# State-space mixer of a perceiver: rows of B, C and x projected one per pair of states and copied a pair later, and the second repeat of x moved forward

## The chip, the cores and the metric

The kernel runs on one core of one Trainium2 chip. A core has TensorE (PE; its weight loads are shown apart as PEld), VectorE (DVE), ScalarE (ACT), GpSimd (POOL) and SyncE (SP), each with a queue of its own that it works off in order. The metric is the device time of one execution in microseconds (us), the median over several runs.

## The reference

The reference is a perceiver of four blocks: cross-attention over a context, self-attention and feed-forward layers of different kinds in turn, on an input of 2 x 256 tokens of width 256. The change lies in one of these layers, a mixer of the Mamba-2 kind:

```python
z, x, Bm, Cm, dtr = jnp.split(hidden_states @ W_in, ..., axis=-1)   # 512, 128, 128, 512, 64
x = silu(causal_conv4(x) + conv_b)
x  = repeat(x as 8 groups of 16, 4)        # 32 groups of 16 channels
Bg = repeat(Bm as 8 groups of 16, 4)       # 16 state columns for each group
Cg = Cm as 32 groups of 16
delta = softplus(dtr @ W_dt + 2.0 * dt_bias)
a  = exp(delta[..., None] * A)             # A = -exp(A_log)
bb = (delta * x)[..., None] * Bg[:, :, :, None, :]
h_t = a_t * h_(t-1) + bb_t                 # for each of 512 channels x 16 states
y  = einsum('blgpn,blgn->blgp', h, Cg)
y  = (y + D * x) * silu(z)
return y @ W_out
```

## The kernel before

The mixer is the function `l1_attn`. Tokens lie along the free axis (512: two batches of 256), channels along the 128 partitions, so the 512 channels make four *quarters* j = 0 to 3. All tiles are f32, and a matmul over 128 x 512 shows as two MATMUL records in the trace.

`project` (L1499) multiplies 128 columns of the input weights with the normed input (two matmuls, four records) into one PSUM bank of the tag "mm"; the tag has three banks, "tr" two, "dec" two and "acc" one. A tile of a tag takes one of the tag's banks, and the first matmul into it waits until the last reader of the bank's former tile is done.

Ahead of the loop stand, in source order: the low-rank steps of quarters 0 and 1 (`steps_of`, bank "dec"), an exponential over both, the Silu of x, the gate z of quarter 0, `repeat_x(0)` (x of quarter 0 spread over its 128 channels by a matmul with a 0/1 matrix, then copied by ScalarE to `xr`), `rows_of_columns(0)` (the rows of B and of C of quarter 0, two projections, each copied by ScalarE, to `bT` and `cT`), the other gates, the softplus polynomial of quarter 0 on VectorE (`deltas(0, True)`), the steps of quarters 2 and 3, their exponential (L1558), `repeat_x(1)` and the polynomial of quarter 1. In this part instructions need not run in source order: each engine's queue is put together by the framework.

Then comes the loop over 32 *pairs* of state columns, eight pairs a quarter. It runs from k = -2 to 32 as a pipeline, and here each engine's order is the one written down (`in_order` over PE, DVE, ACT and POOL). In one turn:

- `states(k)`: PE spreads two columns of C over the partitions into two "mm" banks (L1577, 32-row matmuls that run side by side); VectorE does two scans (L1609) and then multiplies each by its C column (L1611), which frees the bank.
- `b_columns(k + 2)`: PE spreads two columns of B into the two "tr" banks (L1577); ScalarE copies them to `spread` (L1585).
- `drives(k + 1)`: ScalarE makes two decays (L1594) into the two "dec" banks, which the scans of pair k read before; POOL multiplies `spread` by delta times x (L1596). One step of the softplus polynomial of quarters 2 and 3 follows (an addition on ScalarE, L1462, and a multiplication on POOL, L1463).
- one step of `made`, if there is one left: from k = -2 on, in turn rows of B and C of quarter 1, x of quarter 2, rows of quarter 2, x of quarter 3, rows of quarter 3. Each is projected by PE and copied by ScalarE in the same turn (L1533, L1536, L1537); five steps, so done at k = 2.
- `add_up(k - 1)`: PE adds the two weighed states of the pair before to the sum of the quarter (L1618, two full matmuls with the identity).

What needs what was made: B of quarter 1 is first spread at k = 6, C of quarter 1 at k = 8; x of quarter 2 is read by the last softplus step of that quarter at k = 10. Behind the loop the layer ends with a part of the next layer (`conv_hidden`) and the output projection.

Of the kernel before, what the change touches and what calls it, by code (L numbers as in the profile page):

```python
# [22 lines left out]
P = 128  # L23
# [246 lines left out]
class Perceiver:  # L270
# [1197 lines left out]
    def l1_attn(self, x):  # L1468
# [3 lines left out]
        nc = self.nc  # L1472
        T = NT * P
        with ExitStack() as s:
# [24 lines left out]
            def project(at, n):  # L1499
                ps = self.bank([n, T])  # L1500
                self.mm(ps, [(win[:, k, at : at + n], xnT[:, k, :]) for k in range(KC)])
                return ps
# [14 lines left out]
            def steps_of(j):  # L1517
                ps = self.bank([P, T], "dec")
                self.mm(ps, [(wdt[:, ts(j, P)], dtT)])
                nc.scalar.activation(low[:, j, :], ps, AF.Abs, bias=dt2[:, j : j + 1])  # L1520
                nc.scalar.activation(high[:, j, :], ps, AF.Relu, bias=dt2[:, j : j + 1])

            bT, cT = pool.tile([P, 4, T], F32, name="bT"), pool.tile([P, 4, T], F32, name="cT")
            xr = pool.tile([P, 4, T], F32, name="xr")
# [3 lines left out]
            dx, yz = high, low  # L1528

            def repeat_x(j):  # L1530
                ps = self.bank([P, T], "tr")
                self.mm(ps, [(mats["x"][:, ts(j, P)], xc.rearrange("p b l -> p (b l)"))])
                nc.scalar.copy(xr[:, j, :], ps)  # L1533

            def rows_of_columns(j):
                nc.scalar.copy(bT[:, j, :], project(640 + j * P, P))  # L1536
                nc.scalar.copy(cT[:, j, :], project(1152 + j * P, P))  # L1537

            def deltas(j, vector):
                yield from self.softplus(delta[:, j, :], low[:, j, :], high[:, j, :], vector)  # L1540
                engine = nc.vector if vector else nc.gpsimd
                yield lambda: engine.tensor_mul(dx[:, j, :], delta[:, j, :], xr[:, j, :])
# [4 lines left out]
            nc.scalar.activation(xc, xc, AF.Silu, bias=self.col("conv_b"))  # L1547
            steps = [*deltas(0, True)]
            nc.scalar.activation(zs[:, 0, :], project(0, P), AF.Silu)
            repeat_x(0)  # L1550
            rows_of_columns(0)
            for j in range(1, 4):
                nc.scalar.activation(zs[:, j, :], project(j * P, P), AF.Silu)
            for step in steps:
                step()
            steps_of(2)
            steps_of(3)
            nc.scalar.activation(low[:, 2:4, :], low[:, 2:4, :], AF.Exp, scale=-1.0)  # L1558
            repeat_x(1)
            for step in deltas(1, True):  # L1560
                step()
            later = iter([*deltas(2, False), *deltas(3, False)])
            made = iter([partial(f, j) for j in range(1, 4) for f in ([repeat_x] * (j > 1) + [rows_of_columns])])


            pairs = [(j, q, rs) for j in range(4) for q in range(4) for rs in ((0, 1), (2, 3))]
# [13 lines left out]
            def b_columns(k):  # L1580
                got = columns(mats["b"], bT, *pairs[k], "tr")
                spread[k] = []
                for ps in got:
                    spread[k].append(p4.tile([P, T], F32, name="spread", tag="spread"))
                    nc.scalar.copy(spread[k][-1], ps)  # L1585

            def drives(k):
                j, q, rs = pairs[k]
                decay[k], drive[k] = [], []
                for r, b in zip(rs, spread.pop(k)):  # L1590

                    a = fading[len(decay[k])]
                    n = 16 * j + 4 * r + q
                    nc.scalar.activation(behind_first(a), behind_first(delta[:, j, :]), AF.Exp, scale=neg_a[:, n : n + 1])  # L1594
                    decay[k].append(a)
                    nc.gpsimd.tensor_mul(b, dx[:, j, :], b)  # L1596
                    drive[k].append(b)
                step = next(later, None)
                if step is not None:
                    step()  # L1600

            def states(k):
                got = columns(mats["c"], cT, *pairs[k], "mm")
                weighed[k] = []

                for a, bb in zip(decay.pop(k), drive.pop(k)):
                    h = p4.tile([P, T], F32, name="state", tag="state")
                    weighed[k].append(h)
                    nc.vector.tensor_tensor_scan(h, a, bb, 0.0, ALU.mult, ALU.add)  # L1609
                for c, h in zip(got, weighed[k]):  # L1610
                    nc.vector.tensor_mul(h, c, h)  # L1611

            def add_up(k):
                j, q, rs = pairs[k]
                if k % 8 == 0:
                    sums[j] = self.acc([P, T])
                for i, h in enumerate(weighed.pop(k)):
                    nc.tensor.matmul(  # L1618
                        sums[j], self.ident, h, start=k % 8 == 0 and i == 0, stop=k % 8 == 7 and i == 1
                    )  # L1620
                if k % 8 == 7:
                    nc.vector.scalar_tensor_tensor(
                        yz[:, j, :], xr[:, j, :], self.col("ssm_d", j), sums[j], ALU.mult, ALU.add
                    )
                    nc.gpsimd.tensor_mul(yz[:, j, :], yz[:, j, :], zs[:, j, :])

            e = mybir.EngineType
            with self.in_order(e.PE, e.DVE, e.Activation, e.Pool):
                n = len(pairs)
                for a in fading:  # L1630
                    nc.vector.memset(by_batch(a)[:, :, 0:1], 0.0)
                for k in range(-2, n + 1):
                    if 0 <= k < n:
                        states(k)
                    if k + 2 < n:
                        b_columns(k + 2)
                    if 0 <= k + 1 < n:
                        drives(k + 1)
                    step = next(made, None)
                    if step is not None:  # L1640
                        step()
                    if k > 0:
                        add_up(k - 1)
                self.conv_hidden("tr", "tr", "dec")
                return self.linear(yz, wout, x)
# [1248 lines left out]
```

## Time and profile before

| what | value |
|---|---|
| median of 3 runs | 2466.13 us (2465.45 to 2467.29) |
| the profiled execution | 2463.28 us |
| its span (first to last instruction) | 2461.5 us |
| granted TensorE clock, mean over the span | 0.99 |
| the mixer in the span: normed input's first transposes to the last add-up | 1245.6 to 1412.1 us |
| first B columns of the pair loop | 1268.8 us |
| first C columns | 1281.2 us |
| first scan (VectorE) | 1281.3 us |

Busy times of some groups of the mixer:

| line, engine, what | count | busy us | mean ns |
|---|---|---|---|
| L1618 PE, add-up | 128 | 63.3 | 617 |
| L1577 PE, C columns | 128 | 36.6 | 640 |
| L1577 PE, B columns | 128 | 34.9 | 591 |
| L1609 DVE, scan | 64 | 76.3 | 1215 |
| L1611 DVE, multiply by C | 64 | 40.4 | 673 |
| L1585 ACT, copy of a B column | 64 | 34.5 | 589 |
| L1594 ACT, decay | 64 | 42.1 | 698 |
| L1596 POOL, drive | 64 | 80.1 | 1278 |

A group's mean is the duration of a single record. Records of one engine overlap by about a tenth of a microsecond, so the distance between the starts of two instructions, not the mean, says what one costs its engine. In the timeline a row gives start, length of the merged records, engine, line, operation, tiles and the number of records; in brackets the engine's idle time before it, and what ended it.

### The profile page before, as it was taken

The numbers are of one execution on the slowest core, as the hardware profiler recorded it, in microseconds if no ns is written. First come the engines' busy times: TensorE is split into PE (matmuls) and PEld (weight loads), VectorE is DVE, ScalarE is ACT, GpSimd is POOL, SyncE is SP. The second block draws the span as 40 slices with busy tenths as digits, with TensorE's granted clock in tenths as the row PEclk, the third lists the DMA queues.
The fourth block names the chain that finished last, engine by engine and source line by source line (L and its number), as shares of the span: only waits on it lengthen the run. The fifth ranks groups of instructions, "written<-read, shape, count | busy, mean of one in ns | idle before, by whom it ended". The sixth has DMA issues, their size and how long they took to land. (4 is left out here: it accounts for less than half of the span.)

```text
span 2461.5 us, 51429 instructions
## 1 busy us (share of the span) xinstructions
PE 2395.0 (97%) x20501; PEld 1612.3 (66%) x20501; DVE 1676.4 (68%) x3125; ACT 1363.8 (55%) x2588; POOL 916.4 (37%) x860
## 2 busy tenths in 40 slices
PE   8999999999999999999989999999999999999989
PEld 6865577777766666666733376555966666665678
DVE  5645578888877777777758864555258888855642
ACT  3434566666666666666656522433137777785612
POOL 0420066666666655555819722002021222210000
PEclk9999999999999999999999999999999999999989
DMA  8321433333342222222320011125850000004755
GB/s 306 108 88 69 144 91 99 96 99 96 98 131 78 66 67 69 70 70 70 109 106 1 1 77 57 69 82 208 313 184 2 2 2 2 2 2 143 243 221 219
DMA packets 92640, 243.61 MB, mean 99 GB/s; under 512 B 8072, under 2 KB 23248, under 8 KB 81904
## 3 DMA queue, kind: packets, MB, share of 16 engines
q1 hardware_dynamic: 81088, 219.08, 26.7%
q10 hardware_dynamic: 8784, 13.24, 1.5%
q0 software_dynamic: 2528, 8.00, 0.9%
q8 instruction: 162, 2.65, 0.4%
q14 instruction: 78, 0.64, 0.1%
HBM read 206.87 MB, written 33.42 MB: 98 GB/s over the span
## 5 line engine op out<-in xcount | busy, mean ns | idle before, releaser
L1320 POOL TENSOR_TENSOR total<-total,S 128x512 f32<-128x512 f32 x434 | 543.2, 1284 | 227.4 <-ACT S L1309 226.9
L1309 ACT ACTIVATE S<-S 128x512 f32<-128x512 f32 x512 | 304.2, 626 | 209.5 <-DVE S L1306 209.3
L1295 DVE TENSOR_TENSOR most<-ps_mm,most 128x512 f32<-128x512 f32 x448 | 278.1, 683 | 101.1 <-ACT S L1292 101.1
L1306 DVE TENSOR_TENSOR S<-S,ps_dec 128x512 f32<-128x512 f32 x512 | 317.2, 677 | 1.7 <-PE ps_dec L1367 1.7
L2462 DVE TENSOR_REDUCE mx<-ps_mm 128x1 f32<-128x512 f32 x448 | 278.3, 683 | 50.5 <-PE ps_tr L2482 48.6
L1292 ACT COPY S<-ps_mm 128x512 f32<-128x512 f32 x512 | 262.2, 598 | 72.4 <-PE ps_mm L1285 72.4
L2486 ACT ACTIVATE PT<-ps_tr 128x512 f32<-128x512 f32 x476 | 246.8, 601 | 82.2 <-PE ps_tr L2482 78.9
L1238 PEld LDWEIGHTS ps_tr<-w_l1x_wv,ctxT 128*64 128x64 f32 x4096 | 235.5, 137 | 46.3 <-issue 41.7
L1285 PE MATMUL ps_mm<-qT,kT 64*128 64x256 f32 x2048 | 256.6, 389 | 0.0
L1332 PE MATMUL acc<-S,v 128*64 128x256 f32 x2048 | 252.2, 385 | 1.7 <-ACT S L1309 1.0
L1238 PE MATMUL ps_tr<-w_l1x_wv,ctxT 128*64 128x128 f32 x4096 | 248.3, 273 | 0.0
L2482 PE MATMUL ps_tr<-qm,kT 32*128 32x256 f32 x1904 | 240.5, 391 | 0.0
L2458 PE MATMUL ps_mm<-kT,qT 32*128 32x512 f32 x896 | 229.1, 622 | 0.3 <-DVE mx L2462 0.2
L1285 PEld LDWEIGHTS ps_mm<-qT,kT 64*128 64x128 f32 x2048 | 188.3, 186 | 43.9 <-issue 12.8
L1332 PEld LDWEIGHTS acc<-S,v 128*64 128x64 f32 x2048 | 139.5, 136 | 96.2 <-ACT S L1292 33.8
L1238 PE MATMUL ps_tr<-ctxT,w_l1x_wk 128*64 128x512 f32 x800 | 189.6, 593 | 0.0
L2482 PEld LDWEIGHTS ps_tr<-qm,kT 32*128 32x128 f32 x1904 | 173.4, 186 | 16.3 <-issue 6.2
L2507 POOL TENSOR_TENSOR sums<-sums,part 128x256 f32<-128x256 f32 x102 | 73.8, 724 | 250.6 <-ACT part L2506 250.6
L2498 PE MATMUL ps_tr<-PT,v 128*32 128x256 f32 x2048 | 139.4, 385 | 0.3 <-ACT PT L2486 0.3
L336 DVE COPY v<-ps_tr 128x512 f32<-128x512 f32 x120 | 82.4, 687 | 42.6 <-PE ps_tr L1238 42.5
L2458 PEld LDWEIGHTS ps_mm<-kT,qT 32*128 32x128 f32 x896 | 80.4, 186 | 45.0 <-issue 40.7
L1238 PEld LDWEIGHTS ps_tr<-ctxT,w_l1x_wk 128*64 128x64 f32 x800 | 59.7, 137 | 70.5 <-issue 58.8
(587 smaller groups left out, 3848.3 us busy)
## 6 DMA issues: line engine op xcount, KB each, us to landing
ctxT<-in_ctxT SPq DMA_DIRECT2D x144, 512.0 KB, 3.6
w_l2f_gu<-in_l2f_gu SPq DMA_DIRECT2D x16, 1024.0 KB, 5.7
bd_dram<-bd SPq DMA_DIRECT2D x8, 1536.0 KB, 6.7
w_l3f_w<-in_l3f_w SPq DMA_DIRECT2D x11, 1028.0 KB, 8.3
w_l3f_w<-in_l3f_w SPq DMA_DIRECT2D x11, 1024.0 KB, 5.2
ctxT<-in_ctxT SPq DMA_DIRECT2D x8, 1024.0 KB, 6.9
ctx<-in_ctx SPq DMA_DIRECT2D x8, 1024.0 KB, 4.7
ahead_ctx<-in_ctxT SPq DMA_DIRECT2D x8, 1024.0 KB, 7.0
```

The lines of the kernel that those rows point to most:

```text
L1238: nc.tensor.matmul(ps[part], a[:, part], b, start=k == 0, stop=k == len(pairs) - 1)
L1285: nc.tensor.matmul(banks[hh, i][:, j, :], k[part, ts(2 * i + j, P)], q[u][part, :], start=True, stop=True)
L1292: nc.scalar.copy(t, ps)
L1295: nc.vector.tensor_tensor(m, ps, m, ALU.max)
L1306: nc.vector.tensor_tensor(t, t, spread[u][:, hh, :].unsqueeze(1).to_broadcast([P, 2, L]), ALU.add)
L1309: nc.scalar.activation(t, t, AF.Exp)
L1320: nc.gpsimd.tensor_add(tot, tot, t)
L1332: nc.tensor.matmul(av[u][part], vs[:, 2 * i + j, part], got[hh, i][:, j, :], start=g % 8 == 0 and i + j == 0, stop=g % 8 == 7 and i + j == 2,)
L2458: nc.tensor.matmul(ps, qT[rows, 2 * half + c, ts(t, P)], kT[rows, ts(j, 512)], start=True, stop=True,)
L2462: nc.vector.tensor_reduce(mx[:, c, r, j : j + 1], ps, AX.X, ALU.max)
L2482: nc.tensor.matmul(ps[:, i, :], kT[rows, ts(2 * u + i, P)], q[rows], start=True, stop=True)
L2486: nc.scalar.activation(pt, ps, AF.Exp, scale=0.25)
```

## The change

Four things change in `l1_attn`:

- `repeat_x` writes into a "mm" bank in place of a "tr" bank.
- `repeat_x` and the two halves of `rows_of_columns`, now `rows_of_b` and `rows_of_c`, issue only their matmuls when called, and return the copy, to be issued by the caller.
- `repeat_x(1)`, copy included, stands in front of the steps of quarters 2 and 3 and their exponential, instead of behind them.
- In the loop `made` has eight steps instead of five (B 1, C 1, x 2, B 2, C 2, x 3, B 3, C 3) and starts at k = 0 instead of -2, one step a turn, so it is done at k = 7. The copy of a step is issued one turn later, behind `drives` of that turn and in front of the next step.

```diff
             def repeat_x(j):
-                ps = self.bank([P, T], "tr")
+                ps = self.bank([P, T], "mm")
                 self.mm(ps, [(mats["x"][:, ts(j, P)], xc.rearrange("p b l -> p (b l)"))])
-                nc.scalar.copy(xr[:, j, :], ps)
-
-            def rows_of_columns(j):
-                nc.scalar.copy(bT[:, j, :], project(640 + j * P, P))
-                nc.scalar.copy(cT[:, j, :], project(1152 + j * P, P))
+                return partial(nc.scalar.copy, xr[:, j, :], ps)
+
+            def rows_of_b(j):
+                return partial(nc.scalar.copy, bT[:, j, :], project(640 + j * P, P))
+
+            def rows_of_c(j):
+                return partial(nc.scalar.copy, cT[:, j, :], project(1152 + j * P, P))
...
-            repeat_x(0)
-            rows_of_columns(0)
+            repeat_x(0)()
+            rows_of_b(0)()
+            rows_of_c(0)()
...
             for step in steps:
                 step()
+            repeat_x(1)()
             steps_of(2)
             steps_of(3)
             nc.scalar.activation(low[:, 2:4, :], low[:, 2:4, :], AF.Exp, scale=-1.0)
-            repeat_x(1)
...
-            made = iter([partial(f, j) for j in range(1, 4) for f in ([repeat_x] * (j > 1) + [rows_of_columns])])
+            made = iter([partial(f, j) for j in range(1, 4) for f in ([repeat_x] * (j > 1) + [rows_of_b, rows_of_c])])
+            copies = []
...
                     if 0 <= k + 1 < n:
                         drives(k + 1)
-                    step = next(made, None)
+                    while copies:
+                        copies.pop()()
+                    step = next(made, None) if k >= 0 else None
                     if step is not None:
-                        step()
+                        copies.append(step())
                     if k > 0:
                         add_up(k - 1)
```

## The prediction

> **What bounds the kernel now.** I read the page's busy shares first, then the table of busy time by stretch, then the timeline of each engine around the mixer, then its waits.
>
> ```profile
> PE 2395.0 (97%) x20501; PEld 1612.3 (66%) x20501; DVE 1676.4 (68%) x3125; ACT 1363.8 (55%) x2588; POOL 916.4 (37%) x860
> ```
>
> TensorE (PE) is busy nearly everywhere, so a reordering can win only what PE idles, or loses to a lower clock, in the stretch it touches. The pair loop starts at 1268.8 us and its last add-up ends near 1412 us. Split where pair 8 starts (columns: length, busy time of PE, PEld, DVE, ACT, POOL, granted clock, DMA share, GB/s):
>
> ```profile
> 1268.80:1318.90 50.10, 46.67 (x131) 17.09 (x130) 32.11 (x41) 32.34 (x57) 31.66 (x26) 0.97 0.03 11
> 1318.90:1412.00 93.10, 92.71 (x285) 33.56 (x284) 87.59 (x99) 59.11 (x103) 81.35 (x66) 1.00 0.00 1
> ```
>
> Behind 1318.9 PE is full. In front of it PE idles 3.4 us. The timeline of PE says where, and what one pair costs:
>
> ```profile
> 1268.81 1.12 PE L1577 MATMUL ps_tr<-bT,mat_b 32*128 32x512 f32 x2
> 1272.02 1.13 PE L1577 MATMUL ps_tr<-bT,mat_b 32*128 32x512 f32 x2 [2.09 <-ACT xr L1533]
> 1273.09 5.34 PE L359 MATMUL ps_mm<-xT,win 128*128 128x512 f32 x8
> 1280.15 1.12 PE L359 MATMUL ps_tr<-xc,mat_x 128*128 128x512 f32 x2 [0.67 <-ACT spread L1585]
> 1283.41 3.70 PE L359 MATMUL ps_mm<-xT,win 128*128 128x512 f32 x8
> ...
> 1289.69 1.12 PE L359 MATMUL ps_tr<-xc,mat_x 128*128 128x512 f32 x2 [0.67 <-ACT spread L1585]
> ...
> 1307.39 1.13 PE L1577 MATMUL ps_mm<-cT,mat_c 32*128 32x512 f32 x4
> 1308.35 1.02 PE L1577 MATMUL ps_tr<-bT,mat_b 32*128 32x512 f32 x4
> 1309.30 1.98 PE L1618 MATMUL acc<-state,ident 128*128 128x512 f32 x4
> 1311.22 1.13 PE L1577 MATMUL ps_mm<-cT,mat_c 32*128 32x512 f32 x4
> ```
>
> Differences of starts are the costs on PE: C columns 0.96, B columns 0.96, add-up 1.92, so 3.83 us for a pair without a gap. Two projections take 3.63 (1283.41 to 1287.04), one 1.81; a repeated x 0.96. The gaps are 2.09, 0.67 and 0.67. The two projections at 1273.09 took 5.34 instead of 3.70: 1.64 lost to the clock, whose granted share (the column behind PE's busy time) was half here, and full a microsecond before and after:
>
> ```profile
> 1273.00:1274.00 1.00, 1.00 (x2) 0.50 0.00 0
> ...
> 1276.00:1277.00 1.00, 1.00 (x4) 0.79 0.00 0
> ```
>
> So 3.43 of idling, 1.64 of half clock, and about 1 us because pair 0's two B columns ran one after the other instead of side by side: 6 us is the most that can be won. ScalarE and VectorE show the other half:
>
> ```profile
> 1270.44 1.06 ACT L1558 ACTIVATE low<-low 128x1024 f32<-128x1024 f32 x1
> 1271.40 0.57 ACT L1533 COPY xr<-ps_tr 128x512 f32<-128x512 f32 x1
> 1271.87 0.59 ACT L1585 COPY spread<-ps_tr 128x512 f32<-128x512 f32 x1
> 1276.75 0.59 ACT L1536 COPY bT<-ps_mm 128x512 f32<-128x512 f32 x1 [2.96 <-PE ps_mm L359]
> 1280.47 1.31 ACT L1594 ACTIVATE ps_dec<-delta,neg_a 128x510 f32<-128x510 f32 x2
> 1281.28 2.34 DVE L1609 TENSOR_TENSOR_SCAN state<-ps_dec,spread 128x512 f32<-128x512 f32 x2 [8.52 <-ACT ps_dec L1594]
> ```
>
> ScalarE stands behind quarter 1's projections before it can give the first decay, so VectorE's first scan starts 8.52 us late. That costs nothing by itself: VectorE needs two scans and two multiplies, 3.58 to 3.69 us, of PE's 3.83.
>
> **The change, part by part.** No matmul, copy or DMA is added or removed, nothing moves on SP's queue, and PE's work between pair 0 and pair 8 stays six projections and two repeats. What moves:
>
> 1. Repeat of x for quarter 1, from behind the exponential L1558 to in front of quarter 2's steps, and into an "mm" bank. The "tr" bank it held is what the 2.09 gap waited for. On ScalarE its copy (1271.40 to 1271.87, 0.47) leaves the place in front of the first spread copy. Outside the hand-ordered loop the trace is not in source order (quarter 2's steps run before x of quarter 0), so I bound its new place. Early end: the spread copies start when B columns end, 1269.9. Late end: quarter 3's steps slip one slot of 0.96 and with them the exponential, 1272.4. I take 1271.40, where the exponential ends today. Should the exponential land between the Silu activations, its table load (1.28, as at L1546) comes again in front of the first decay, which eats the 1.5 of the early end.
>
> 2. Nothing is projected at k = -2 and -1. From the rows: spread copies of pair 0 at 1271.40 and 1271.88, first "tr" bank free at 1272.0, B columns of pair 1 at 1272.05. PE idles 2.28 from 1269.77, the same gap as today, so I let the clock halve from 1273.0 to 1276.2 again. Spreads of pair 1 at 1273.12, decays of pair 0 at 1274.08, first scan at 1274.84 (6.4 earlier). On PE C columns of pair 0 start at 1273.0 and, at half clock, B columns of pair 2 at 1274.9, the first projection at 1277.0 to 1278.8.
>
> 3. One projection a pair, at k = 0 to 7, copied a pair later. The copies sit on ScalarE behind the next spreads (0.96 for two), decays (1.24) and the addition of L1462 (0.52): 3.22 with the copy's 0.50, hidden in a pair of 0.96 + 0.96 + 1.81 + 1.92 = 5.64 on PE. Without that cover the eight copies would cost 8 x 0.50 = 4.0.
>
> 4. The new wait. A pair now takes all three "mm" banks: two for C columns, one for the projection. The projection at k must find a bank, and queued behind it on PE are the add-up and the next C columns, for which VectorE's multiply waits. If it gets whichever bank comes free first, that is the first C column's, after the multiply. At k = 1: scans 1278.38 to 1280.62, first multiply done 1281.29, projection at 1281.35, PE idle 0.61. From k = 2 on PE arrives later than the multiply (0.13 lost at two places). The other end, the bank of the projection before, is rival 1.
>
> Walking on: pair 2 starts at 1285.07; then x 4.79, B 5.77, C 5.64, x 4.79, B 5.77, C 5.64 gives 1317.5 for pair 8, against 1318.88 today. From there both run 3.83 a pair on PE. Sum: -1.4 us.
>
> [...]
>
> **How the sum stands to the runs.** It is worked out in one execution of 2463.28 us (span 2461.5), 2.85 below the median of 2466.13. Taken off the median: 2464.7.
>
> Its own bounds: the early end of part 1 gives -1.4 - 1.5 = -2.9; the late end +1.0 - 1.4 = -0.4, or +1.0 where the half clock then delays B columns of pair 2 and with them the spreads; a second half-clock stretch after the 0.61 gap adds 1.6. So -3 to +3: 2463 to 2469.
>
> **Rivals.**
>
> Rival 1, the bank (slower). Each projection gets the bank of the one before it. Then PE stands at k = 1 to 7 until ScalarE has made the late copy, and the chain closes on itself: projection 1.81, add-up 1.92, C columns 0.96, B columns to first copy 1.05, spreads 0.96, decays 1.24, addition 0.52, copy 0.59, release 0.05: 9.1 instead of 5.64, seven times 3.46 = 24.2, less 1.4: 2466.1 + 22.8 = 2488.9. It decides from 1281 us on. For it: three banks, three tiles a pair, and a copy behind eight ScalarE operations. Against it: the C bank is free 1 to 3 us sooner, and in the trace projections have waited for VectorE's multiply (two waits, 1.0 us in all), so they do take banks of C columns.
>
> Rival 2, late and cold (a little slower). The start slips beyond the late end by another table load (1.28) and the gap at k = 1 halves the clock again (1.6): +1.0 + 1.3 + 1.6 = 3.9, at most 6: 2467 to 2472. For it: 2.09 us idle did it before. Against: 0.67 twice did not.
>
> Rival 3, everything hidden (faster). The spreads start at once, PE never waits long enough for the clock to fall, and of the 6 us some 5 are won: 2461.1. Against it: the deltas of quarter 0 end on VectorE at 1271. Even with the first decay there, the first scan follows 0.8 later, the scans take 2.24 and one multiply 0.67: C banks come free at 1274.7, and those of pair 1 another 0.6 + 2.24 + 0.67 later, at 1278.2, when PE has been without work since 1276.6 (two columns of 0.96 behind 1274.7). These 1.6 leave 4.4 of the 6, unless the projection at k = 1 finds another bank.
>
> **Chances.** Forecast 0.58, rival 1 0.20, rival 2 0.12, rival 3 0.10. A measurement of this kernel tells 0.2%, or 4.9 us, from no change. Below 2461.2: most of rival 3, 0.07. Above 2471.1: rival 1 and half of rival 2, 0.27. Between: 0.66. The range 2461 to 2472 leaves out rival 1.
>
> **What would show it.** First scan near 1275 (step 2); no wait for xr in front of pair 0's second B column (step 1); pairs 2 to 7 at 5.6 or 4.8 us with PE's projections not waiting for bT, cT or xr copies (step 4); pair 8 near 1317.5, then 3.83. Gaps of 3 us in front of seven projections, ended by ScalarE, would make the prediction wrong, as would a start of the loop shifted from 1268.8.

## The result and the profile after

The changed kernel takes **2472.07 us** (median of 20 runs, 2466.35 to 2478.24), the kernel before, measured beside it, 2466.57 (20 runs, 2464.37 to 2470.68). The ratio is 1.0020, with a 95% interval of 1.0014 to 1.0027: slower by some 5.5 us. The profiled execution took 2473.93 us (span 2472.1).

In what follows the *mixer* is the stretch on TensorE (PE) from the first transpose of the normed input to the first matmul behind the last add-up. It is 166.40 us in the trace of before (from 1245.63) and 172.77 in that of after (from 1246.40): 6.4 longer. The spans of these two executions differ by 10.6; the other 4.2 lie in code that the change doesn't touch (0.8 ahead of the mixer, 3.4 behind it), so the change is read in the mixer. The page's busy shares hardly tell it:

```profile
PE 2400.9 (97%) x20501; PEld 1615.1 (65%) x20501; DVE 1677.5 (68%) x3125; ACT 1366.5 (55%) x2590; POOL 915.9 (37%) x860
```

PE is busy 5.9 us more with the same 20501 matmuls: they ran slower, at a lower clock (0.988 granted over the span, 0.990 in before). ScalarE (ACT) has two instructions more, 2590 for 2588. The table by stretch (columns: length, busy time of PE, PEld, DVE, ACT, POOL, granted clock, DMA share, GB/s), cut where the first B columns of the loop start and where pair 8 starts:

```profile
1246.40:1274.59 28.19, 25.92 (x53) 10.30 (x53) 18.34 (x32) 17.80 (x24) 0.00 (x0) 0.82 0.46 169
1274.59:1326.03 51.44, 48.60 (x130) 18.79 (x129) 31.00 (x37) 31.49 (x55) 33.14 (x27) 0.93 0.00 0
1326.03:1419.17 93.14, 92.75 (x285) 33.62 (x284) 85.99 (x98) 58.58 (x102) 79.69 (x65) 1.00 0.00 1
```

In before the first two stretches took 23.18 (clock 0.93) and 50.07 (0.97). So 5.0 us are lost **ahead of the loop**, which the prediction had left as it was, and 1.4 in its first eight pairs. From pair 8 to the mixer's end nothing is lost (93.14, before 93.15). The timeline of PE, after:

```profile
1256.88 1.98 PE L359 MATMUL ps_dec<-dtT,w_l1a_wdt 64*128 64x512 f32 x4
1261.10 2.08 PE L359 MATMUL ps_mm<-xc,mat_x 128*128 128x512 f32 x2 [2.24 <-ACT xc L1549]
1262.97 10.83 PE L359 MATMUL ps_mm<-xT,win 128*128 128x512 f32 x20
1273.64 1.02 PE L359 MATMUL ps_mm<-xc,mat_x 128*128 128x512 f32 x2
1274.59 1.13 PE L1581 MATMUL ps_tr<-bT,mat_b 32*128 32x512 f32 x4
1276.39 1.18 PE L1581 MATMUL ps_tr<-bT,mat_b 32*128 32x512 f32 x2 [0.67 <-ACT spread L1589]
1276.88 0.70 PE L1581 MATMUL ps_mm<-cT,mat_c 32*128 32x512 f32 x2
...
1279.72 1.98 PE L359 MATMUL ps_mm<-xT,win 128*128 128x512 f32 x4
1283.70 1.81 PE L1581 MATMUL ps_mm<-cT,mat_c 32*128 32x512 f32 x3 [1.99 <-DVE state L1615]
...
1288.00 3.48 PE L359 MATMUL ps_mm<-xT,win 128*128 128x512 f32 x4
1291.32 1.88 PE L1622 MATMUL acc<-state,ident 128*128 128x512 f32 x4
```

Two waits stand there, each with slow matmuls behind it. The repeat of x of quarter 0 (first row with a wait) now stands in front of the projections of quarter 0's rows and of the other three gates, and PE waits 2.24 us for the Silu that makes its input. In the trace of before it stood behind the projections of the first gate and of quarter 0's rows, and nothing waited:

```profile
1254.10 5.42 PE L359 MATMUL ps_mm<-xT,win 128*128 128x512 f32 x12
1259.44 1.12 PE L359 MATMUL ps_dec<-dtT,w_l1a_wdt 64*128 64x512 f32 x2
1260.50 1.12 PE L359 MATMUL ps_tr<-xc,mat_x 128*128 128x512 f32 x2
1261.46 5.31 PE L359 MATMUL ps_mm<-xT,win 128*128 128x512 f32 x12
1266.70 1.12 PE L359 MATMUL ps_dec<-dtT,w_l1a_wdt 64*128 64x512 f32 x2
```

In after the 20 records behind the repeat (five projections) take 10.7 us from start to start. At 1.81 a projection they would take 9.1; at 1.75, as the three from 1261.46 on in before, 8.7. Further down, C columns of pair 1 wait 1.99 us until VectorE's first multiply (L1615) gives back a bank, after which a projection takes 3.48 instead of 1.98. The granted clock (the column behind PE's busy share) in slices of a microsecond:

```profile
1259.00:1260.00 1.00, 0.00 (x0) 1.00 0.23 37
1260.00:1261.00 1.00, 0.00 (x0) 0.66 0.87 258
1261.00:1262.00 1.00, 0.90 (x1) 0.50 0.57 229
...
1267.00:1268.00 1.00, 1.00 (x3) 0.92 0.00 0
...
1283.00:1284.00 1.00, 0.30 (x1) 1.00 0.00 0
1284.00:1285.00 1.00, 1.00 (x3) 0.61 0.00 0
...
1291.00:1292.00 1.00, 1.00 (x3) 0.98 0.00 0
```

With each of the two waits come some 6.8 us at half clock, worth 3.4 us (one minus the granted clock, summed over the slices). Before had one stretch worth 1.7. This leaves out what every kernel here loses in the first five us of its mixer, 1.6 to 1.7; so do the figures that follow. ScalarE's timeline, after:

```profile
1266.63 0.59 ACT L1553 COPY bT<-ps_mm 128x512 f32<-128x512 f32 x1 [1.66 <-PE ps_mm L359]
1267.23 1.28 ACT L1562 ACT_TABLE_LOAD   x1
1268.53 1.06 ACT L1562 ACTIVATE low<-low 128x1024 f32<-128x1024 f32 x1
1269.49 0.57 ACT L1554 COPY cT<-ps_mm 128x512 f32<-128x512 f32 x1
1270.07 1.28 ACT L1556 ACT_TABLE_LOAD   x1
...
1278.64 1.28 ACT L1598 ACT_TABLE_LOAD   x1
1279.93 1.30 ACT L1598 ACTIVATE ps_dec<-delta,neg_a 128x510 f32<-128x510 f32 x2
```

The exponential of quarters 2 and 3 now runs in front of three gates' Silus, so the table is loaded twice more. The last load stands directly in front of the first decay. VectorE's first scan starts at 1280.72, 6.1 after the first B columns.

### The profile page after: what moved, and what is told of

It is laid out like the page before. It is cut to its first block, busy times and chain, and to the rows that moved or that the text cites. A ratio compares the mean times of both kernels' runs of the same rounds, so it can differ in the third digit from the quotient of the medians.

```text
span 2472.1 us, 51430 instructions
## 1 busy us (share of the span) xinstructions
PE 2400.9 (97%) x20501; PEld 1615.1 (65%) x20501; DVE 1677.5 (68%) x3125; ACT 1366.5 (55%) x2590; POOL 915.9 (37%) x860
```

## The experiments

All times are medians beside runs of the kernel before on the same chip. "Ahead" is the time from the mixer's start to the first B columns, "half clock" the loss to the lower clock within the mixer, as above; all in us. The last column is the 95% interval of the ratio to the time of before. The lengths within the mixer come from one trace each.

| run | ahead | mixer | mixer against before | half clock | time against before | ratio, 95% |
|---|---|---|---|---|---|---|
| before | 23.18 | 166.40 | | 1.7 | | |
| after | 28.19 | 172.77 | +6.4 | 6.8 | +5.5 | 1.0014 to 1.0027 |
| e1_x0_tr | 22.90 | 168.34 | +1.9 | 5.1 | +4.2 | 1.0009 to 1.0027 |
| e2_x0_mm | 28.30 | 168.81 | +2.4 | 3.4 | +3.2 | 1.0003 to 1.0020 |
| e3_loop | 23.14 | 168.66 | +2.3 | 5.1 | +8.3 | 1.0011 to 1.0035 |
| e4_x1_early | 22.88 | 161.28 | -5.1 | 0 | -5.5 | 0.9969 to 0.9987 |
| e5_filled | 22.90 | 166.17 | -0.2 | 0 | +0.8 | 0.9999 to 1.0017 |
| e6_from_first | 22.95 | 167.76 | +1.4 | 3.4 | +0.5 | 0.9999 to 1.0017 |
| e7_x1_and_mm | 23.07 | 159.80 | -6.6 | 0 | -6.3 | 0.9961 to 0.9982 |
| e8_x0_behind_rows | 23.32 | 168.97 | +2.6 | 5.1 | -0.2 | 0.9988 to 1.0012 |
| e9_start_alone | 28.00 | 167.76 | +1.4 | 3.4 | -0.6 | 0.9987 to 1.0012 |

Where the time and the mixer disagree (e3, e8, e1) the rest of the span differs too. Half-clock stretches come and go there in code that no kernel here changes: the profile of e3 loses 5.1 us to one from 1648 to 1659, that of before none at that place. Over the whole span e3's trace loses some 10 us more to half clock than before's, about as much as its span is longer (10.3). Mechanisms are therefore read in the mixer, and the medians say whether a difference is more than that scatter.

**e1_x0_tr: the changed kernel with x of quarter 0 back in a "tr" bank.**

```diff
-            def repeat_x(j):
-                ps = self.bank([P, T], "mm")
+            def repeat_x(j, tag="mm"):
+                ps = self.bank([P, T], tag)
...
-            repeat_x(0)()
+            repeat_x(0, "tr")()
```

> The changed kernel with x of quarter 0 alone back in a "tr" bank. The mixer's length is counted on TensorE from the first transpose of the normed input to the first matmul behind the last add-up: 166.4 us before, 172.8 in the changed kernel, of which 5.0 lie ahead of the first B columns and 1.4 behind them. Theory (the bank of x(0) put it ahead of the rows of B and C in TensorE's queue, where it waits for the Silu): those 5.0 us go, TensorE has no gap of 2.2 us there, the mixer is 165 to 168 us and the time -2 to +2 us against the kernel before. Rival (the later projections in the loop cost the time): the mixer stays above 170 us and the time +4 us or more.

One word takes the 5.0 us ahead of the loop away. The mixer and the time stay above what was expected (168.3 us, +4.2): the loop now loses more (145.4 us from the first B columns on, 144.6 in after, 143.2 before), and the time is longer by more than the mixer. Its PE timeline shows where:

```profile
1268.25 1.13 PE L1581 MATMUL ps_tr<-bT,mat_b 32*128 32x512 f32 x4
1272.52 1.70 PE L1581 MATMUL ps_tr<-bT,mat_b 32*128 32x512 f32 x2 [3.14 <-ACT spread L1589]
```

With the start recovered, the spread copies wait on ScalarE behind the exponential, PE has nothing else to do, and the clock is at half for 10 us behind it (slices of a microsecond):

```profile
1272.00:1273.00 1.00, 0.48 (x1) 0.77 0.00 0
1273.00:1274.00 1.00, 1.00 (x5) 0.50 0.00 0
...
1282.00:1283.00 1.00, 1.00 (x4) 0.61 0.00 0
```

**e2_x0_mm: the kernel before with x of quarter 0 alone in a "mm" bank.**

```diff
-            def repeat_x(j):
-                ps = self.bank([P, T], "tr")
+            def repeat_x(j, tag="tr"):
+                ps = self.bank([P, T], tag)
...
-            repeat_x(0)
+            repeat_x(0, "mm")
```

> The kernel before with one word changed: x of quarter 0 in an "mm" bank. Theory: the same queue ahead of the loop as in the changed kernel, a gap of about 2.2 us in front of x(0), two more table loads on ScalarE; from first transpose to first B columns 28 us instead of 23.2; mixer 171 to 173 us, time +4.5 to +6.5 us against before. Rival (the loop): nothing, within 1 us of before.

The loss ahead of the loop comes with that word alone, +5.1 us, with the same wait on PE:

```profile
1260.41 2.08 PE L359 MATMUL ps_mm<-xc,mat_x 128*128 128x512 f32 x2 [2.23 <-ACT xc L1547]
1262.28 10.87 PE L359 MATMUL ps_mm<-xT,win 128*128 128x512 f32 x20
```

Half of the loss comes back: in this order the 2.09 us gap at the loop's start and its half clock are gone, so the mixer (168.8) is only 2.4 longer and the time 3.2, both less than expected.

**e8_x0_behind_rows: the changed kernel with x of quarter 0 written behind quarter 0's rows, still in a "mm" bank.**

```diff
-            repeat_x(0)()
             rows_of_b(0)()
             rows_of_c(0)()
+            repeat_x(0)()
```

> The changed kernel with x of quarter 0 written behind quarter 0's rows of B and C, still in an mm bank; nothing else differs, and the loop is the changed one. In TensorE's queue the repeat of x then stands behind B's and C's rows instead of in front of them. Theory (the place in the queue costs, not the bank): no wait for the Silu in front of x, at most 0.5 us; from the mixer's first transpose to the first B columns 22.9 to 23.4 instead of 28.2; no half clock in front of the loop; the loop then costs what it cost with x of quarter 0 back in a tr bank (145.4): mixer 168 to 169; time +2 to +5 against before. Rival (the mm bank itself is what x waits for, or the exponential still slips between the Silus and its two table loads are the cost): the wait of about 2.2 comes again behind the rows, or 25 to 28 stay ahead of the loop.

The place in the queue it was, and not the bank: the same repeat into the same tag waits for nothing behind the rows.

```profile
1260.04 1.98 PE L359 MATMUL ps_dec<-dtT,w_l1a_wdt 64*128 64x512 f32 x4
1261.95 1.12 PE L359 MATMUL ps_mm<-xc,mat_x 128*128 128x512 f32 x2
1262.92 5.31 PE L359 MATMUL ps_mm<-xT,win 128*128 128x512 f32 x12
```

The early exponential and its two further table loads are still in this trace (at 1265.53, 1267.89 and 1273.55), with 23.32 us ahead of the loop. So the two loads cost at most 0.4 us there (e1 has 22.90 without them). The loop costs 145.7, as in e1; the mixer's +2.6 is as expected, while the time, -0.2 us with a spread of 2459.69 to 2474.28, is below what was expected and does not show it.

**e4_x1_early: the kernel before with x of quarter 1 alone moved forward, still in a "tr" bank.**

```diff
+            repeat_x(1)
             steps_of(2)
             steps_of(3)
...
-            repeat_x(1)
             for step in deltas(1, True):
```

> The kernel before with x of quarter 1 alone moved in front of the steps of quarters 2 and 3, in its "tr" bank. Theory: the wait of 2.09 us for its copy goes, with it the half clock (1.6 us) and the B columns of pair 0 one after the other (1 us), while the projections still fill TensorE at k = -2 and -1: mixer 162 to 164.5 us, time -2 to -4.8 us against before. Rival (the wait only moves, to the spread copies of pair 0 or to the first decay): mixer 165.5 to 167 us, time within 1 us.

This part of the change alone wins 5.5 us, more than expected and close to the 6 that the prediction named as the most. B columns of pair 0 run side by side, the two projections that still belong to k = -2 stand behind them, and the clock stays full.

```profile
1267.72 1.13 PE L1577 MATMUL ps_tr<-bT,mat_b 32*128 32x512 f32 x4
1268.78 3.70 PE L359 MATMUL ps_mm<-xT,win 128*128 128x512 f32 x8
```

**e3_loop: the changed loop alone, with the start as before.** Against the changed kernel:

```diff
-            repeat_x(0)()
+            repeat_x(0, "tr")()
...
-            repeat_x(1)()
             steps_of(2)
...
+            repeat_x(1, "tr")()
             for step in deltas(1, True):
```

> The loop's part of the change alone: ahead of the loop everything as before, x of quarters 0 and 1 in "tr" banks and x(1) behind the exponential; in the loop one projection a pair from k = 0, copied a pair later. Theory: 23.2 us ahead of the first B columns as before; the 2.09 us wait for the copy of x(1) stays, and the projections that filled TensorE behind it are gone, so the loop wins nothing: mixer 166 to 168.5 us, time -0.5 to +2 us. Rival (the loop costs the time): mixer above 170 us, +4 us or more.

The 2.09 us gap stays, as before. Behind it the clock now loses three units of 1.7 us instead of one; only columns and one projection follow, and the projection takes 3.78 us instead of 1.98:

```profile
1272.19 3.08 PE L1581 MATMUL ps_tr<-bT,mat_b 32*128 32x512 f32 x5 [2.09 <-ACT xr L1562]
...
1278.79 3.78 PE L359 MATMUL ps_mm<-xT,win 128*128 128x512 f32 x4
```

The mixer is 2.3 longer, just above what was expected. The time is 8.3 longer, of which the mixer explains 2.3. The stretch at 1648 to 1659 in this profile, 5.1, is outside the changed code; e4's profile has one of the same size from 1637 to 1648, so it isn't this kernel's alone, and why it comes in these two and not in the others is open.

**e5_filled: e1 with three matmuls into a spare bank at k = -2.** Nothing reads what they compute.

```diff
+                    if k == -2:
+                        spare = self.acc([P, T])
+                        for _ in range(3):
+                            self.mm(spare, [(mats["x"][:, 0:P], xc.rearrange("p b l -> p (b l)"))])
                     while copies:
```

> As e1 (the changed kernel, x of quarter 0 in a "tr" bank), with three matmuls of 128 x 512 added at k = -2 behind the B columns of pair 0, into the accumulator's bank, read by nobody: 2.9 us of work in the place of the 3.14 us gap. Theory (the gap itself is harmless, the half clock of about 10 us behind it costs): the clock stays full behind the gap and the mixer comes down from 168.3 to 165 to 166.7 us although TensorE does more. Rival (what costs is the wait for VectorE and ScalarE, which the clock only fills): the mixer stays at 168 us or rises, TensorE idles elsewhere.

The strongest sign of what the clock costs in the loop: 2.84 us of useless work on the engine that bounds the kernel, and the mixer is 2.2 us *shorter* than in e1.

```profile
1269.26 2.84 PE L359 MATMUL acc<-xc,mat_x 128*128 128x512 f32 x6
1272.47 1.18 PE L1581 MATMUL ps_tr<-bT,mat_b 32*128 32x512 f32 x2 [0.37 <-ACT spread L1589]
```

The gap shrinks from 3.14 to 0.37 and no half clock is left behind it. So what the projections at k = -2 gave was, besides their work, a running clock.

**e6_from_first: e1 with the steps begun at k = -2, one a pair, copied late.**

```diff
-                    step = next(made, None) if k >= 0 else None
+                    step = next(made, None)
```

> As e1, with the eight steps begun at k = -2 instead of 0, still one a pair and copied a pair later. Theory (what the loop loses is the filling of TensorE while ScalarE makes the first spreads and decays): no gap above 1.5 us and no half clock behind pair 0, mixer 161.5 to 164 us, time -2 to -5 us against before. Rival (one step a pair with a late copy costs by its waits for banks): mixer above 166 us and gaps in front of the projections.

This expectation was missed: the mixer takes 167.8, the time is +0.5. One projection covers only part of the gap (1.23 remains), and now the late copy does hold a bank: C columns of pair 1 wait 0.79 us for it, and the clock falls: the projection behind them takes 3.78 us instead of 1.98.

```profile
1282.10 0.69 PE L1581 MATMUL ps_mm<-cT,mat_c 32*128 32x512 f32 x1 [0.79 <-ACT cT L1644]
```

**e7_x1_and_mm: e4 with x of quarters 2 and 3 in "mm" banks.**

```diff
-                ps = self.bank([P, T], "tr")
+                ps = self.bank([P, T], "tr" if j < 2 else "mm")
```

> As e4 (the kernel before with x of quarter 1 early), and x of quarters 2 and 3 in an "mm" bank, those of quarters 0 and 1 left in "tr". The two gaps of 0.61 and 0.67 us in front of x(2) and x(3), which wait for a spread copy, go: mixer 160 to 161 us, time -5 to -7 us against before. Rival: the bank is missed by the C columns behind, the gap moves there, mixer 161.3 us or more.

The two waits for a spread copy in front of these repeats (0.61 and 0.67 in e4) go, and the loop up to pair 8 is without any idling, at full clock:

```profile
1268.71:1312.31 43.60, 43.60 (x130) 15.85 (x129) 31.94 (x41) 32.47 (x57) 31.55 (x26) 1.00 0.03 13
```

The mixer is 6.6 shorter, a little more than the 6 that the prediction named as the most. This kernel beats both others: 2457.17 us (8 runs, 2455.35 to 2458.83) against 2463.46 of before on that chip.

**e9_start_alone: the changed start with the loop as before.** Against the changed kernel:

```diff
-            def repeat_x(j):
-                ps = self.bank([P, T], "mm")
+            def repeat_x(j, tag="mm"):
+                ps = self.bank([P, T], tag)
...
-            made = iter([partial(f, j) for j in range(1, 4) for f in ([repeat_x] * (j > 1) + [rows_of_b, rows_of_c])])
+            made = iter([partial(f, j) for j in range(1, 4) for f in ([lambda j: [repeat_x(j, "tr")]] * (j > 1) + [lambda j: [rows_of_b(j), rows_of_c(j)]])])
...
-                    step = next(made, None) if k >= 0 else None
+                    step = next(made, None)
                     if step is not None:
-                        copies.append(step())
+                        for c in step():
+                            c()
```

> The fourth corner: the changed kernel's work ahead of the loop (x of quarters 0 and 1 in mm banks, quarter 1's early), with the loop as before (both rows in a step from two pairs ahead, copied at once, x of quarters 2 and 3 in tr banks). Theory (two separate costs that add up): 28.2 ahead of the first B columns with the 2.2 wait for the Silu and half clock near 1260 to 1268; the loop as in the kernel with x of quarter 1 alone moved, 138.4 from there, with no half clock; mixer 166 to 167.5, so -1 to +1 against before's 166.4 and the time within 2 us of before. Rival (the late start itself makes the loop slow, by a clock that has not recovered): mixer 169 or more, half clock again between 1270 and 1290, time +3 or more.

28.0 ahead and then no half clock, but 139.8 from the first B columns, 1.4 more than expected: one more wait of 0.58 us for the copy of xr, and one B column after the other at that place. The new start by itself comes out near zero: what x of quarter 1 wins (5.1), x of quarter 0 gives back.

**r_after: the changed kernel once more.**

> The changed kernel as it is, looked at a second time, since the runs of one kernel lie up to 12 us apart. Theory (the spread is that of the stretches of half clock, which come or stay away with the position of the gaps): mixer 170 to 174 us again with the gap of 2.2 us in front of x(0) and the wait for the C banks, and the difference to the first look a multiple of about 1.7 us of half clock, anywhere in the span. Rival (something else varies): the spans differ by other things than the clock.

Ahead 28.24, mixer 172.83, the same four gaps and half clock 6.8: the mixer's structure repeats. The span is 3.3 us shorter than in the first trace; one unit of half clock, 1.7, is missing behind the mixer (near 1830), and the other 1.6 stay open. The one time, 2470.59 us, stands 7.1 over the median of before on that chip.

## Why the prediction was wrong

It put pair 8 at 1317.5; in after it starts at 1326.03, or at 1325.3 if the 0.77 us by which this mixer starts later are taken off. Of these 7.8 us the later start of the loop makes 5.0 and the pairs up to 8 make 2.7.

**Step 1 failed, and with it the sum.** It followed the repeat of quarter 1 and took the work ahead of the loop as fixed, up to the first B columns at 1268.8. The same edit puts the repeat of quarter 0 into a "mm" bank, among the tiles of rows and gates, and that repeat then stands in front of quarter 0's rows and of the other gates in PE's queue, as the source has it. In its "tr" bank it had stood behind the rows. The trace of before showed that order, against the source, and the prediction noted that this part is not in source order; it did not ask what the order depended on. e2 shows that the one word brings the loss, e1 that taking it back removes it, e8 that it is the place in the queue. Why the framework orders by tag was not tested. In the traces the tiles of one tag run in source order ahead of the loop, as far as their readers show it, and only tiles of different tags pass each other. In all three kernels that have quarter 0's repeat in a "mm" bank and in front of the rows in the source (after, e2, e9), it runs in front of them. Price: 2.24 of waiting and 2.5 to 2.9 of half clock (1.6 to 1.9 on the five projections, 0.9 on the repeat, which takes 1.87 from start to start for 0.96). The prediction named a shifted start as what would make it wrong. This step is not the whole miss: e1, without the loss, still has a mixer 1.9 longer than before, where the sum has 1.4 less.

For quarter 1's repeat itself the early end came true: the first spread copy runs 1.2 us behind the first B columns (1275.75 against 1274.59), and the further table load falls in front of the first decay, as step 1 said of that case. The first scan stands 6.1 behind the first B columns; 6.0 was predicted, from the middle case, and the agreement comes from the early end and the load offsetting each other.

**Step 2 put the gap in the wrong place and mis-sized the half clock.** It let B columns of pair 1 wait 2.28 us, with one half-clock stretch of 1.6. They waited 0.67, at full clock. PE therefore came to C columns of pair 1 earlier, when VectorE's first multiply was not done, and stood 1.99 us there. The loss to half clock behind it was 3.4, and 5.1 in e1, e3 and e8. The prediction took a stretch of before's length, though in before eight records of full-size projections followed the gap, and in the changed loop the 32-row columns do; whether that makes the difference was not tried by itself. e5 shows the clock's own part: 2.2 us of e1's loop come back when it stays up.

The larger part lies in the new order of the loop itself. The step measured itself against before, whose loop had a wait and a half clock of its own. e7 takes as long ahead of the loop as e1 (23.07 and 22.90) and leaves the projections of the loop where they were; quarter 1's repeat, early in both, has a "tr" bank in e7 and a "mm" bank in e1. From the first B columns on e7 takes 136.7 us, e1 145.4. Of the 8.7 between them 3.3 are idling of PE and 5.1 half clock. With the clock kept up by useless matmuls (e5) the loop is still 6.5 longer than in e7: 2.8 are those matmuls and 1.6 waits of PE, and the rest was not taken apart. With the changed start, too, the changed loop costs 4.8 (144.6 in after, 139.8 in e9).

**Step 3 held**: in after no matmul waits for a late copy. e6 shows how near it is: with the steps two pairs earlier one of them holds a bank for 0.79 us.

**Step 4 held in its main point, not at k = 1.** The projections take the bank that comes free first; from pair 2 on none waits, and pairs 2 to 7 took 32.9 us where 32.4 was predicted. In e5 and e8 the projection at k = 1 waits for VectorE's multiply as the step said, 0.85 us in each. In after its 0.61 us at k = 1 became the 1.99 just told, in front of C columns instead of the projection. So rival 1 (the bank of the projection before) did not happen.

Rival 2 had half the mechanism, the second halving of the clock at k = 1, at 3.9 us and at most 6. Its condition was not met: the start did not slip beyond the late end (6.1, as just told), and the further load in front of the first decay only used up what the early end had won. The wait came because PE was there sooner. That its upper end, 2472, lies at the measured time is chance, since 5.0 of the loss lie ahead of the loop. The 5 us of rival 3 are there to be won, as e4 and e7 show, but with the projections left where they were.

One slip in the chances: rival 1 and half of rival 2 make 0.26, where the prediction has 0.27.

## What to carry to other kernels

Where a framework makes the queues, moving a tile to another group of buffers can move its instructions too: ask for every caller of the edited function where it will stand in its queue, and what it waits for there. Work that seems to be in the way in front of a pipeline may be useful work that TensorE can do while the pipeline fills, and what keeps its clock up there (e5: 2.84 us of matmuls in that place took the half clock from the 5.1 us of e1 to none); here the start did best with all its projections left in (e4, e7). And an edit with several parts deserves a run of each part alone: one word of this change cost 5 us ahead of the loop, and one moved line, in the kernel before, won 5.

## What the runs showed of the hardware

Losses to the lower clock within the mixer came in units of about 1.7 us, that is 3.4 us at a granted clock of 0.50: 0, 1.7, 3.4, 5.1 or 6.8. The slices taken of the mixer (of one or two us) show 0.50 or 1.00, and a value between only where one passes into the other. In after the clock falls or rises at 1246.68, 1250.08, 1260.32, 1267.16, 1284.22 and 1291.04 (worked out from the slices: one of 0.66 from 1260 on puts the fall at 1260.32); the distances are 1, 3, 2, 5 and 2 times 3.41 us. In before, e1, e8 and e9 they come out as whole multiples of it as well: 3.4, 23.9 and 3.4 in before, 3.4, 23.9 and 10.2 in e1, 3.4, 23.9, 3.4, 3.4 and 6.8 in e8, 3.4, 10.2 and 6.8 in e9.

The clock fell during the wait of 2.24 us in after, 0.5 us behind that of 1.99 there and 1.0 behind that of 2.09 in before; in e8 it fell behind waits of 1.15 and 0.17 with 32-row matmuls between them. The length of a wait alone does not decide: in e8, from 1277.8 to the second fall at 1281.2, PE had a wait of 0.34, the last half microsecond of a projection and otherwise columns of 32 rows, while in e5 the clock stayed full through waits of 0.58 and 0.85 (1277.8 to 1281.8).

It was not expected that the clock stays at half while PE is busy in nearly every slice, for 10 us in e1. There the work was columns of 32 rows and one projection; in before, with eight records of projections behind a gap of 2.09, it was back after 3.4. That the size of the matmuls decides this fits these runs but was not tried by itself.
